# Two queues that fetch single rows: more rows for ScalarE and SyncE, and the rows' offsets loaded earlier

## The chip, the core and the metric

The kernel runs on one core of one Trainium2 chip. Its metric is the device time of one launch in microseconds (us); less is better. Five engines work side by side and meet through semaphores: PE (matrix products), DVE (vector work), ACT (ScalarE: activations), POOL (GpSimd: here it issues gathers by a list of indices) and SP (SyncE: it only issues DMAs). ACT issues DMAs too. Each engine takes its instructions in the program's order.

## What is computed

A recommender's attention over a user's items. For each of B = 16384 users there are 69 item numbers and one label; every number picks a row of 96 floats of a table of 100001 rows. For each of the 69 items the row u, the label's row q and their products go through a small gated layer that gives one weight. The weighted rows are summed in ten groups, and a three-layer network on these sums gives one number for each user.

```python
u = emb[batch_user]                       # 16384 x 69 rows of 96
ql = emb[batch_label[:, 0]]
q = jnp.broadcast_to(ql[:, None, :], u.shape)
z = jnp.concatenate([q, u, q - u, q * u], axis=-1)
h = _dice(z @ W1 + b1, a1, EPS_DICE)      # (alpha * (1 - p) + p) * x, p = sigmoid(x)
att = (h @ W2 + b2) @ W3 + b3
pre = jnp.where(eff, u * att, 0.0)        # eff: batch_user < ITEM_NUM
pooled = jnp.einsum('gf,bfe->bge', window, pre).reshape(u.shape[0], G * E)
x = jnp.concatenate([pooled, ql], axis=-1)
h = _dice(_bn_eval(x @ Wf1 + bf1, EPS_BN), af1, EPS_DICE)
h = _dice(_bn_eval(h @ Wf2 + bf2, EPS_BN), af2, EPS_DICE)
return h @ Wf3 + bf3
```

So 16384 x 69 rows of 384 bytes, picked at random places, have to come from HBM.

## The kernel before, in words

The rows are worked on in chunks of 512: four *tiles* of 128 rows, one row in each partition. There are 32 blocks of 512 users with 69 chunks each, 2208 chunks in all, and the program is written out in 1104 *steps* of two chunks. A table of steps (`plan`, L592) holds what is issued in which step; `at(step, work)` adds to it, and each engine's order follows from the order in which the steps are written out.

In step i the order is: the attention rows of earlier pairs (`rows_of`, every fourth step), the tail chunks of pair i - 3, the spread of weights (every fourth step), the hidden layer of pair i - 2 (`hidden`, L389), ACT's single rows (`scalar_rows`, L610), the pooling of pair i - 7 (`pool`, L448) and the fetch of pair i (`fetch`, L359). A pair's rows stay in one of 15 buffers u (L134) from the fetch until they are pooled, seven steps later.

- **Gathers.** For each tile of a chunk POOL issues one indirect DMA (L266) with 128 indices. PE transposes the tile into PSUM (`ptr`, L325), DVE copies it out (`uT`, L376) and multiplies it by q (`quT`, L379 or L386).
- **The gate.** In `hidden` PE makes `ph` (L396 to L403). ACT makes the sigmoid of it into y (L405) and then `y * (1 - a1) + a1` in place (L406, the identity), and DVE multiplies by `ph` (L407). In the next step PE reads y for the attention rows (`prow`, L414) or a tail (`pa`, L423).
- **Single tiles.** Some tiles, always the fourth of a chunk (`SLOT = 3`), don't go through POOL. Their rows are fetched one by one: `dma_start` of 384 bytes for one partition of a buffer of `ring` (L301). SP fetches 199 such tiles, ACT 170. `SP_CHUNKS` (L52) and `ACT_CHUNKS` (L55) say in which chunk each is read: SP's tile s in step int(5.5 s) + 6, ACT's in step (s + 1) * 128 // 20 + 2. PE waits for the rows by a semaphore of the tile (L320) and then reads the ring's buffer instead of u, for the transpose and again for the pooling. POOL issues no gather for it.
- **The offsets.** The row numbers of single tiles lie in SBUF as byte offsets (`offsets`, L156 to L159). `load` (L283) brings 32 of them at a time into registers of the issuing engine by one instruction (L286, TENSOR_LOAD in the profile), just before the first of the 32 rows that use them. Each row is then a MOVE and a DMA on the engine's queue.
- **When they are issued.** SP's tile s is put into the plan in step int(5.5 s), whole: 128 rows. SP runs free of the steps otherwise: it only waits until the buffer of the ring (eight for SP) has been read out by the pooling of the tile eight before. ACT's rows are spread: 20 in each step, behind the gate's two activations, into a ring of four buffers.

Of the kernel before, what the change touches and what calls it, by code (L numbers as in the profile page):

```python
# [18 lines left out]
P = 128  # L19
# [29 lines left out]

ROW_BYTES = 4 * E  # L50
SLOT = 3
SP_CHUNKS = [2 * (int(5.5 * s) + 6) + 1 for s in range(199)]  # L52
SP_RING = 8
ACT_ROWS = 20
ACT_CHUNKS = [2 * ((s + 1) * P // ACT_ROWS + 2) for s in range(170)]  # L55
ACT_RING = 4
SINGLES = SP_CHUNKS + ACT_CHUNKS
NSB = (len(SINGLES) + P - 1) // P
NSEM = 8
RING_BYTES = 4096  # L60


def chunk_of(c):

    n, k = divmod(c, NCH)
    if n == NBLK - 1 and k >= EARLY:
        k = NMAIN + k - EARLY if k < EARLY + NTAIL else k - NTAIL
    return n, k
# [47 lines left out]
def rec_kernel(  # L116
# [13 lines left out]
    row_bytes = rows.bitcast(U8).rearrange("(o n) k -> o (n k)", o=1)  # L130
# [144 lines left out]
    class Singles:  # L275

        def __init__(self, name, engine, kind, chunks, first, buffers, group):
            self.name, self.engine, self.kind, self.group = name, engine, kind, group
            self.chunks, self.first, self.buffers = chunks, first, buffers
            self.sems = [tc.alloc_semaphore(f"{name}{k}") for k in range(NSEM)]  # L280
            self.given = [0] * NSEM

        def load(self, s, start):  # L283

            i, stop = self.first + s, min(P, start + self.group)
            _, values = nc.values_load_multi_w_load_instructions(  # L286
                offsets[i % P : i % P + 1, i // P, start:stop],
                engines=[self.kind],
                min_val=0,
                max_val=ITEM_NUM * ROW_BYTES,  # L290
                skip_runtime_bounds_check_because="offsets of rows of the table",
            )
            self.values = dict(enumerate(values, start))

        def fetch(self, s, start, stop):

            b, k = self.buffers[s % len(self.buffers)], s % NSEM
            for r in range(start, stop):
                if r % self.group == 0:
                    self.load(s, r)  # L300
                d = self.engine.dma_start(  # L301
                    out=ring[r : r + 1, b], in_=row_bytes[:, bass.ds(self.values[r], ROW_BYTES)]
                ).then_inc(self.sems[k], 16)
                tc.no_tile_sem_insts.add(d.ins.name)
                tc.declare_no_dep(d.ins, group=f"ring{b}", reason="a buffer's readers have waited for its rows")
                fresh.setdefault(b, []).append(d.ins)
            if stop == P:
                for ins in fresh.pop(b):
                    tc.add_to_no_dep_group(f"ring{b}", ins)
                self.given[k] += 16 * P  # L310
                places[self.chunks[s]] = b, self.sems[k], self.given[k]
# [74 lines left out]
                nc.vector.tensor_tensor(quT[:, j, :], ptr, q[:, 0:BLK], ALU.mult)  # L386
        return u, uT, quT

    def hidden(i, uT, quT):  # L389

        ph = ps_h.tile([P, 512], F32, tag="h", name=f"ph{i}")
        places = [chunk_of(2 * i + j) for j in range(2)]
        sums = [ph[j * H1 : (j + 1) * H1, :] for j in range(2)]
        for (n, k), p in zip(places, sums):
            if k >= NMAIN:
                nc.tensor.matmul(p, Cq, qTs[n % 2], start=True, stop=False)  # L396
        for j, ((n, k), p) in enumerate(zip(places, sums)):
            if k < NMAIN:
                nc.tensor.matmul(p, As[n % 2][:, k // 4, :], uT[j], start=True, stop=False)  # L399
            else:  # L400
                nc.tensor.matmul(p, A, uT[j][0:E], start=False, stop=False)  # L401
        for j, p in enumerate(sums):
            nc.tensor.matmul(p, Wp, quT[:, j, :], start=False, stop=True)  # L403
        y = ypool.tile([P, 512], F32, tag="y", name=f"y{i}")
        nc.scalar.activation(y, ph, AF.Sigmoid, scale=S_DICE)  # L405
        nc.scalar.activation(y, y, AF.Identity, bias=a1c, scale=na1c)  # L406
        nc.vector.tensor_mul(y, ph, y)  # L407
        return y
# [131 lines left out]
    pooled, pres, x1s, x2s, qs, us, hs, ys, bands, rws, p1s = ({} for _ in range(11))  # L540
# [26 lines left out]
    def hidden_of(k):  # L567
        return lambda: ys.__setitem__(k, hidden(k, *hs[k]))
# [25 lines left out]
    def at(step, *work):  # L594
        plan.setdefault(step, []).extend(work)

    by_sync = Singles("sp", nc.sync, mybir.EngineType.SP, SP_CHUNKS, 0, range(SP_RING), 32)
    for s, m in enumerate(SP_CHUNKS):
        at(max(0, m // 2 - 6), lambda s=s: by_sync.fetch(s, 0, P))

    by_scalar = Singles(
        "act",
# [1 line left out]
        mybir.EngineType.Activation,  # L604
        ACT_CHUNKS,
        len(SP_CHUNKS),
        range(SP_RING, SP_RING + ACT_RING),
        32,
    )
    def scalar_rows(i):  # L610

        row, stop = i * ACT_ROWS, min((i + 1) * ACT_ROWS, len(ACT_CHUNKS) * P)
        while row < stop:
            s, start = divmod(row, P)
            n = min(P - start, stop - row)
            by_scalar.fetch(s, start, start + n)
            row += n

    c = NPAIR - CLOSE
    for i in range(c):  # L620
        if i >= 3 and (i - 3) % 4 == 3:
            at(i, rows_of(i - 6, 4))
        if i >= 3:
            at(i, tails_of(i - 3))
        if i >= 4 and (i - 4) % 4 == 3:
            at(i, spread_of(i - 7, 4))
        if i >= 2:
            at(i, hidden_of(i - 2))
        at(i, lambda i=i: scalar_rows(i))
        if i < c - CLOSE:  # L630
            if i >= POOL_LAG:
                at(i, pool_of(i - POOL_LAG))
        else:

            for k in {0: (-15, -14), 1: (-13,), 3: (-12, -11), 4: (-10, -9), 7: (-8, -7)}.get(i - c + 8, ()):
                at(i, pool_of(c + k))
        at(i, fetch_of(i))

    at(c, pool_of(c - 6), pool_of(c - 5), tails_of(c - 3), hidden_of(c - 2), fetch_of(c))
# [8 lines left out]
    for n in range(NBLK):  # L648
        first, end = n * NCH // 2, ((n + 1) * NCH - 1) // 2
# [104 lines left out]
```

## Time and profile before

| | |
|---|---|
| time, median of three runs | 16508.57 us (16477.51 to 16532.16) |
| span of the profiled execution, first to last instruction | 10780.4 us |
| between that span and the median | 5728.2 us |
| PE busy | 81% |
| POOL busy | 75% |
| DVE busy | 39% |
| ACT busy (activations alone) | 17% |
| granted clock of PE, mean | 0.749 |
| gathers of u that POOL issues | 8463 |
| single rows issued by SP and by ACT | 25472 and 21760 |

The page gives the span of the profiled execution and no other time of it. The busy shares of POOL and of PE are shares of that span. Instructions that only issue a DMA, move a register or load one are not counted as busy, so SP has no share at all, and ACT's leaves out everything that it issues for the single tiles; their lengths are read from the timeline. The 40 slices of the page are alike from the second to the last but one: there is one stage.

### The profile page before, as it was taken

To read this page: it belongs to the slowest core of one execution; us is meant where nothing else is said; L and a number is where in the kernel's file an instruction comes from. 1 tells how busy PE (TensorE), PEld (TensorE's weight loads), DVE (VectorE), ACT (ScalarE), POOL (GpSimd) and SP (SyncE) were. 2 spreads that over 40 slices of the span, in tenths; PEclk is the share of its full clock that TensorE was granted. 3 is DMA by queue.
4 is the path that set the end of the run, shared out by engine and by line. 5 is a ranking of instruction groups with operands and counts; after the bars stand their busy time and mean duration, and the time that the engine had idled before them with its cause. 6 is when DMAs were issued, how large, how long until landed. Compare 5 with 4: busy or idle time off the path is not lost.

```text
span 10780.4 us, 204439 instructions
## 1 busy us (share of the span) xinstructions
PE 8756.9 (81%) x41797; PEld 4310.8 (40%) x41797; DVE 4235.1 (39%) x7535; ACT 1884.4 (17%) x2761; POOL 8110.8 (75%) x8597
## 2 busy tenths in 40 slices
PE   6888888888887788877888788888887887888888
PEld 3434444434433344433433344333343343443335
DVE  4333333333333333333333343333333334333333
ACT  1111111111111111111111111111111111111112
POOL 7777777777777777777777777777777777777776
PEclk7777777677777777777777777777777777777778
DMA  2222222222222222222222222222222222222221
GB/s 50 42 42 42 45 42 42 42 42 45 42 42 42 45 42 42 42 42 45 42 42 42 42 44 42 42 42 42 44 42 42 42 42 44 42 42 42 42 42 34
DMA packets 372495, 460.70 MB, mean 43 GB/s; under 512 B 232114, under 2 KB 232626, under 8 KB 371106
## 3 DMA queue, kind: packets, MB, share of 16 engines
q0 software_dynamic: 274912, 422.81, 18.9%
q1 hardware_dynamic: 52802, 16.36, 1.0%
q10 hardware_dynamic: 43520, 8.44, 0.7%
q14 instruction: 925, 7.58, 0.2%
q8 instruction: 336, 5.51, 0.2%
HBM read 446.81 MB, written 0.07 MB: 41 GB/s over the span
## 4 chain that ended last, share of the span: by engine, by line
POOL 40%; PE 21%; issue 19%; DMA 12%; ACTq 6%; ACT 2%; DVE 1%; POOLq 0%
POOL u L266 40%; DMA u<-in_rows,ids 12%; ACTq L301 4%; PE acc L325 4%; PE p L502 4%; PE ph L399 3%; PE ph L403 3%; PE ptr L325 2%; PE prow L414 1%; ACTq L286 1%; PE pa L423 1%; ACT y L405 1%; POOL q L266 1%; PE ph L396 1%; PE ph L401 1%
## 5 line engine op out<-in xcount | busy, mean ns | idle before, releaser
L266 POOL DMA_INDIRECT u<-in_rows,ids x8463 | 7989.1, 944 | 2583.5 <-issue 2389.6
L325 PE MATMUL ptr<-ident,u 128*96 128x128 f32 x8463 | 1925.1, 332 | 1606.1 <-DMA u<-in_rows,ids 1555.6
L407 DVE TENSOR_TENSOR y<-ph,y 128x512 f32<-128x512 f32 x1104 | 763.5, 692 | 4972.6 <-ACT y L406 4699.0
L325 PEld LDWEIGHTS acc<-rw,u 128*96 128x96 f32 x15702 | 1674.4, 188 | 1332.5 <-issue 840.4
L325 PEld LDWEIGHTS ptr<-ident,u 128*96 128x96 f32 x8463 | 1131.6, 151 | 2282.7 <-DMA u<-in_rows,ids 1853.2
L325 PE MATMUL acc<-rw,u 128*96 128x20 f32 x15702 | 1792.0, 259 | 212.0 <-DVE rw L436 177.6
L376 DVE COPY uT<-ptr 96x512 f32<-96x512 f32 x2208 | 1489.0, 674 | 739.9 <-PE ptr L325 737.5
L405 ACT ACTIVATE y<-ph 128x512 f32<-128x512 f32 x1104 | 658.8, 597 | 6119.1 <-PE ph L403 3304.1
L399 PE MATMUL ph<-uT,A 128*64 128x512 f32 x4096 | 1598.9, 856 | 0.0
L403 PE MATMUL ph<-quT,wn 96*64 96x512 f32 x4416 | 1540.5, 767 | 0.0
L379 DVE TENSOR_TENSOR quT<-ptr,qT 96x512 f32<-96x512 f32 x2048 | 1379.1, 673 | 0.0
L406 ACT ACTIVATE y<-y,wn,na1c 128x512 f32<-128x512 f32 x1104 | 897.9, 813 | 36.6
L403 PEld LDWEIGHTS ph<-quT,wn 96*64 96x64 f32 x4416 | 429.4, 183 | 1002.5 <-issue 1001.8
L502 PE MATMUL p<-pooled,wf 96*100 96x512 f32 (+1 forms) x1400 | 667.7, 624 | 0.0
L414 PE MATMUL prow<-y,v 128*32 128x512 f32 x2208 | 507.2, 885 | 65.4 <-DVE y L407 57.6
L399 PEld LDWEIGHTS ph<-uT,A 128*64 128x64 f32 x4096 | 259.6, 172 | 609.6 <-issue 605.5
L416 ACT COPY row<-prow 128x512 f32<-128x512 f32 (+1 forms) x277 | 161.6, 583 | 1733.2 <-issue 675.0
L470 DVE COPY pooled<-acc 96x160 f32<-96x160 f32 x1008 | 420.5, 417 | 99.1 <-PE acc L325 97.6
L502 PE MATMUL p<-pre,V 96*100 96x512 f32 (+1 forms) x700 | 398.0, 714 | 11.1 <-DVE x L485 10.8
L502 PEld LDWEIGHTS p<-pooled,wf 96*100 96x100 f32 x1400 | 249.6, 190 | 316.5 <-issue 316.5
L436 DVE SCALAR_TENSOR_TENSOR rw<-patt,bb,wn 128x320 f32<-128x320 f32 x554 | 276.1, 539 | 116.8 <-PE patt L431 114.7
L485 DVE SCALAR_TENSOR_TENSOR x<-p,wf,g 100x512 f32<-100x512 f32 (+3 forms) x105 | 73.9, 704 | 523.6 <-ACT g L484 523.5
(72 smaller groups left out, 2706.1 us busy)
## 6 DMA issues: line engine op xcount, KB each, us to landing
ring<-in_rows SPq DMA_DIRECT2D x25472, 0.4 KB
ring<-in_rows ACTq DMA_DIRECT2D x21760, 0.4 KB
u<-in_rows,ids POOLq DMA_INDIRECT x8463
ids<-in_idx SPq DMA_DIRECT2D x8, 560.0 KB, 3.9
q<-in_emb,ids POOLq DMA_INDIRECT x128
wf<-in_far SPq DMA_DIRECT2D x1, 1209.0 KB, 8.3
wn<-in_near SPq DMA_DIRECT2D x1, 236.0 KB, 3.4
offsets<-in_single_rows SPq DMA_DIRECT2D x1, 192.0 KB, 2.5
```

The lines of the kernel that those rows point to most:

```text
L266: nc.gpsimd.indirect_dma_start(out=dst, out_offset=None, in_=table, in_offset=bass.IndirectOffsetOnAxis(ap=index, axis=0),)
L301: d = self.engine.dma_start(out=ring[r : r + 1, b], in_=row_bytes[:, bass.ds(self.values[r], ROW_BYTES)]).then_inc(self.sems[k], 16)
L325: ins = op(out, ring[:, at[0]].bitcast(F32) if at else u[:, 4 * (c % 2) + t, :], other, **how)
L376: nc.vector.tensor_copy(uT[j][0:E], ptr)
L379: nc.vector.tensor_tensor(quT[:, j, :].rearrange("e (s f) -> e s f", f=FM), ptr.rearrange("e (s f) -> e s f", f=FM), by_field(q[:, k * NS ...
L399: nc.tensor.matmul(p, As[n % 2][:, k // 4, :], uT[j], start=True, stop=False)
L403: nc.tensor.matmul(p, Wp, quT[:, j, :], start=False, stop=True)
L405: nc.scalar.activation(y, ph, AF.Sigmoid, scale=S_DICE)
L406: nc.scalar.activation(y, y, AF.Identity, bias=a1c, scale=na1c)
L407: nc.vector.tensor_mul(y, ph, y)
L414: nc.tensor.matmul(pr[32 * k : 32 * (k + 1), :], v2, ys[b + k], start=True, stop=True)
L502: nc.tensor.matmul(p1, w[:, h * DH : (h + 1) * DH], x, start=(k == 0), stop=(k == KTOP - 1))
```

## The change

Four things are altered, all of them on the single tiles.

- `SP_CHUNKS`: a tile every 5.3 steps instead of 5.5, read 8 steps after it is put into the plan instead of 6; 206 tiles instead of 199.
- `ACT_CHUNKS`: 23 rows a step instead of 20, tiles read 5 steps after their last row's step instead of 2, a ring of 8 buffers instead of 4; 195 tiles instead of 170.
- `load` is called eight rows before the first row that uses its registers (`EARLY_LOAD`), not just before it. The registers of the last eight rows stay valid until then.
- `hidden` takes work that is issued between the gate's two activations: the first four of the step's 23 rows on ACT. The other 19 stand where the 20 stood.

```diff
-SP_CHUNKS = [2 * (int(5.5 * s) + 6) + 1 for s in range(199)]
+SP_STEPS = 5.3
+SP_AHEAD = 8
+SP_CHUNKS = [2 * (int(SP_STEPS * s) + SP_AHEAD) + 1 for s in range(206)]
 SP_RING = 8
-ACT_ROWS = 20
-ACT_CHUNKS = [2 * ((s + 1) * P // ACT_ROWS + 2) for s in range(170)]
-ACT_RING = 4
+ACT_ROWS = 23
+ACT_FIRST = 4
+ACT_AHEAD = 5
+ACT_CHUNKS = [2 * ((s + 1) * P // ACT_ROWS + ACT_AHEAD) for s in range(195)]
+ACT_RING = 8
+EARLY_LOAD = 8
...
             for r in range(start, stop):
-                if r % self.group == 0:
-                    self.load(s, r)
+                g = s * P + r
+                if g == 0:
+                    self.load(0, 0)
+                if (g + EARLY_LOAD) % self.group == 0 and g + EARLY_LOAD < P * len(self.chunks):
+                    self.load(*divmod(g + EARLY_LOAD, P))
...
-    def hidden(i, uT, quT):
+    def hidden(i, uT, quT, between=None):
...
         nc.scalar.activation(y, ph, AF.Sigmoid, scale=S_DICE)
+        if between:
+            between()
         nc.scalar.activation(y, y, AF.Identity, bias=a1c, scale=na1c)
...
-        at(max(0, m // 2 - 6), lambda s=s: by_sync.fetch(s, 0, P))
+        at(max(0, m // 2 - SP_AHEAD), lambda s=s: by_sync.fetch(s, 0, P))
...
-    def scalar_rows(i):
+    def scalar_rows(i, first, last):
 
-        row, stop = i * ACT_ROWS, min((i + 1) * ACT_ROWS, len(ACT_CHUNKS) * P)
+        row, stop = (min(i * ACT_ROWS + n, len(ACT_CHUNKS) * P) for n in (first, last))
...
         if i >= 2:
-            at(i, hidden_of(i - 2))
-        at(i, lambda i=i: scalar_rows(i))
+            at(i, hidden_of(i - 2, lambda i=i: scalar_rows(i, 0, ACT_FIRST)))
+        at(i, lambda i=i: scalar_rows(i, ACT_FIRST if i >= 2 else 0, ACT_ROWS))
```

On ACT's queue, in the middle of the program before: y is the gate's buffer, offsets the loaded row numbers, and the last number of a row DMA's line how many stand one behind the other.

```order
L405 ACTIVATE y_32405<-ph_32400 128x512
L406 ACTIVATE y_32405<-y_32405,wn,na1c 128x512
L301 DMA ring<-in_rows 1x384 x12
L286 TENSOR_LOAD offsets
L301 DMA ring<-in_rows 1x384 x8
L416 COPY row_32523<-prow_32518 128x512
L405 ACTIVATE y_32530<-ph_32525 128x512
L406 ACTIVATE y_32530<-y_32530,wn,na1c 128x512
L301 DMA ring<-in_rows 1x384 x20
```

And two steps of the same stretch now (L311, L292, L415 and L418 are the new numbers of L301, L286, L405 and L406):

```order
L415 ACTIVATE y_33622<-ph_33615 128x512
L311 DMA ring<-in_rows 1x384 x4
L418 ACTIVATE y_33622<-y_33622,wn,na1c 128x512
L311 DMA ring<-in_rows 1x384 x9
L292 TENSOR_LOAD offsets
L311 DMA ring<-in_rows 1x384 x10
L428 COPY row_34141<-prow_34136 128x512
L415 ACTIVATE y_34155<-ph_34149 128x512
L311 DMA ring<-in_rows 1x384 x4
```

Four rows stand between sigmoid and identity, and 19 behind the identity. On SP's queue at the start of the program the loads stood like this, each directly before the 32 rows that use it:

```order
L164 DMA wf<-in_far 128x2418
L286 TENSOR_LOAD offsets
L301 DMA ring<-in_rows 1x384 x32
L286 TENSOR_LOAD offsets
L301 DMA ring<-in_rows 1x384 x32
```

Now the second load stands behind 24 rows, and so on with 32 rows between two loads:

```order
L169 DMA wf<-in_far 128x2418
L292 TENSOR_LOAD offsets
L311 DMA ring<-in_rows 1x384 x24
L292 TENSOR_LOAD offsets
L311 DMA ring<-in_rows 1x384 x32
```

Behind each load but the first there are eight rows whose registers were loaded earlier. The number of loads is one for 32 rows, as before.

More of the change, by code (lines that the diff above doesn't have):

```diff
@@ L281, in __init__ @@
             self.given = [0] * NSEM
+            self.values = {}
         def load(self, s, start):
@@ L292, in load @@
             )
-            self.values = dict(enumerate(values, start))
+            self.values = {g: v for g, v in self.values.items() if g >= s * P + start - self.group}
+            self.values.update(enumerate(values, s * P + start))
         def fetch(self, s, start, stop):
@@ L298, in fetch @@
             for r in range(start, stop):
-                if r % self.group == 0:
-                    self.load(s, r)
+                g = s * P + r
[3 more added lines that the diff above has]
+                    self.load(*divmod(g + EARLY_LOAD, P))
                 d = self.engine.dma_start(
-                    out=ring[r : r + 1, b], in_=row_bytes[:, bass.ds(self.values[r], ROW_BYTES)]
+                    out=ring[r : r + 1, b], in_=row_bytes[:, bass.ds(self.values[g], ROW_BYTES)]
                 ).then_inc(self.sems[k], 16)
@@ L565, in pool_of, with hidden_of @@
         return lambda: pool(k)
-    def hidden_of(k):
-        return lambda: ys.__setitem__(k, hidden(k, *hs[k]))
+    def hidden_of(k, between=None):
+        return lambda: ys.__setitem__(k, hidden(k, *hs[k], between))
     def tails_of(k):
```

## The prediction

> **What bounds the kernel now.** I read the page first, then the groups of GpSimd's instructions, then the waits.
>
> ```profile
> span 10780.4 us, 204439 instructions
> PE 8756.9 (81%) x41797; PEld 4310.8 (40%) x41797; DVE 4235.1 (39%) x7535; ACT 1884.4 (17%) x2761; POOL 8110.8 (75%) x8597
> ```
> ```profile
> L266 POOL DMA_INDIRECT u<-in_rows,ids x8463 | 7989.1, 944 | 2583.5 <-issue 2389.6 <-DMA u<-in_rows,ids 79.4 <-PE ptr L325 78.8
> L266 POOL DMA_INDIRECT q<-in_emb,ids x128 | 121.0, 946 | 40.6 <-issue 38.8 <-DMA ids<-in_idx 1.8
> ```
> ```profile
> POOL u L266 <- issue: 2389.6, 7828, 0.3
> PE ptr L325 <- DMA u<-in_rows,ids: 1555.6, 1927, 2.2
> ```
> By busy share PE leads with 81% and POOL has 75%. The share misleads. A u gather takes 0.944 us and is followed by a pause that is never longer than 0.3 us (the last number of the first wait row), so nothing that the kernel does holds POOL up: it issues without a stop. Busy and idle of the u row make 7989.1 + 2583.5 = 10572.6 us, or 10572.6 / 8463 = 1.249 us for each gather. With the q row (121.0 + 40.6) POOL's gathers fill 10734.2 of the 10780.4 us; 46.2 us are start and tail. PE, with all its work, waits 1555.6 us for gathers to land: 1555.6 / 1104 = 1.41 us in a step. POOL's issue is the bound, and its length is the number of gathers times 1.249 us.
>
> SP and ACT carry single tiles of 128 rows past POOL, one DMA a row. How near are these two queues to their own limit?
>
> ```profile
> 6.74 48.92 SPq L301 DMA_DIRECT2D ring<-in_rows  x128
> ...
> 1189.62 1284.26 SPq L301 DMA_DIRECT2D ring<-in_rows  x3200
> 2474.51 0.37 SPq L151 DMA_DIRECT2D ids<-in_idx  x1
> 2477.15 2.86 SPq L301 DMA_DIRECT2D ring<-in_rows  x9
> ```
> ```profile
> 79.65 0.27 PE L325 MATMUL ptr<-ident,ring 128*96 128x128 f32 x1
> ```
> ```profile
> 10342.04 0.42 PE L325 MATMUL ptr<-ident,ring 128*96 128x128 f32 x1
> ```
> In these rows (start, length, engine) SP works 2477.15 - 1189.62 = 1287.53 us on 25 tiles without a stop: 51.50 us a tile, with its four loads of offsets. PE reads SP's tile 0 (step 6) at 79.65 and tile 192 (step 1062) at 10342.04, so a step lasts 10262.39 / 1056 = 9.718 us, and SP is asked for a tile every 5.5 x 9.718 = 53.45 us. It gains about 2 us a tile.
>
> For ACT, four steps in the middle:
>
> ```profile
> 5003.38 0.60 ACT L405 ACTIVATE y<-ph 128x512 f32<-128x512 f32 x1 [7.97 <-PE ph L403]
> 5004.01 0.81 ACT L406 ACTIVATE y<-y,wn,na1c 128x512 f32<-128x512 f32 x1
> 5004.08 9.05 ACTq L301 DMA_DIRECT2D ring<-in_rows  x20
> 5013.17 0.58 ACT L416 COPY row<-prow 128x512 f32<-128x512 f32 x1 [8.34 <-issue]
> 5015.05 0.60 ACT L405 ACTIVATE y<-ph 128x512 f32<-128x512 f32 x1 [1.30 <-PE ph L403]
> 5015.68 0.81 ACT L406 ACTIVATE y<-y,wn,na1c 128x512 f32<-128x512 f32 x1
> 5015.75 6.37 ACTq L301 DMA_DIRECT2D ring<-in_rows  x20
> 5022.22 0.60 ACT L405 ACTIVATE y<-ph 128x512 f32<-128x512 f32 x1 [5.72 <-PE ptr L325]
> 5022.85 0.81 ACT L406 ACTIVATE y<-y,wn,na1c 128x512 f32<-128x512 f32 x1
> 5022.92 8.85 ACTq L301 DMA_DIRECT2D ring<-in_rows  x20
> 5031.87 0.60 ACT L405 ACTIVATE y<-ph 128x512 f32<-128x512 f32 x1 [8.20 <-PE ph L403]
> ```
> ```profile
> L416 ACT COPY row<-prow 128x512 f32<-128x512 f32 (+1 forms) x277 | 161.6, 583 | 1733.2 <-issue 675.0 <-PE prow L414 487.8 <-PE ptr L325 315.8
> L484 ACT ACTIVATE g<-g,dice,dice 100x512 f32<-100x512 f32 (+3 forms) x105 | 81.5, 776 | 3.5
> L483 ACT ACTIVATE g<-p,dice 100x512 f32<-100x512 f32 (+3 forms) x105 | 68.1, 649 | 732.7 <-issue 248.8 <-PE p L502 166.2 <-PE ptr L325 131.6
> L349 ACT COPY A<-pc 32x512 f32<-32x512 f32 x64 | 35.2, 576 | 248.9 <-issue 127.7 <-PE pc L348 121.2
> ```
> ```profile
> L301 SPq DMA_DIRECT2D ring<-in_rows x25472: 227/228/482, 6.7 to 10349.8; - x199
> L301 ACTq DMA_DIRECT2D ring<-in_rows x21760: 213/214/587, 18.6 to 10606.0; - x200
> ```
> ```profile
> L286 SPq TENSOR_LOAD <-offsets x796: 2025/2176/2410, 4.5 to 10337.5; - x199
> L286 ACTq TENSOR_LOAD <-offsets x680: 2105/2274/2522, 16.3 to 10592.8; - x170
> ```
> Twenty rows without a load take ACT's queue 5022.22 - 5015.75 = 6.47 us, 0.3235 us a row; with a load 5013.17 - 5004.08 = 9.09 and 5031.87 - 5022.92 = 8.95 us, so a load adds 2.55 us. From the sigmoid's start to the first row pass 5004.08 - 5003.38 = 0.70 us in which the queue issues nothing. Summed: 21760 x 0.3235 = 7039, 680 x 2.55 = 1734, 1104 x 0.70 = 773, and 161.6 + 81.5 + 68.1 + 35.2 = 346 for the other activations: 9892 us. ACT's busy share of 17% hides a queue that is 92% full.
>
> **The change part by part.** The sum goes against the profiled execution: its span of 10780.4 us. The median of the runs shown is 16508.57 us, so 5728.2 us lie around the span which no row shows. I take them as constant.
>
> *32 more single tiles.* SP 206 instead of 199, ACT 195 instead of 170: POOL issues 8431 u gathers instead of 8463. 32 x 1.249 = **-40.0 us**, all on the path, since POOL never waits. PE's work is the same, its operand lies in another buffer. SP's and ACT's 4096 added row DMAs run beside POOL as long as both queues keep up. That has to be shown for each, with the new step of 9.718 x 8559 / 8591 = 9.682 us.
>
> *SP, a tile per 5.3 steps.* It is asked for a tile every 5.3 x 9.682 = 51.31 us and needs 51.50 us at the old prices. Its tile 0 is read two steps later than before, at 79.65 + 2 x 9.682 = 99.0, its last (205, step 1094) at 99.0 + 1086 x 9.682 = 10613.7. SP would finish at 6.74 + 206 x 51.50 = 10615.7: about 2 us late at the very end and nowhere else. PE has ten steps left there, in each of which it now waits 1.41 us for POOL, so up to 14 us of lateness is made up: **0 us** in the sum. If this cover goes, each 0.1 us on SP's tile costs 206 x 0.1 = 20.6 us.
>
> *Offsets loaded eight rows sooner.* The load row is 2176 ns (SP) for 32 registers, 68 ns each, and the row DMAs behind a load wait for it: ACT's twenty rows take 2.55 us longer with one, its own row says 2274 ns. Two readings are open. If the sequencer itself is held for the length of the load, its place doesn't matter and nothing is won: 0. If only the first use of a register is held, eight rows of 0.32 us (2.6 us) cover the whole load and SP gains 4 x 2.18 = 8.7 us a tile, ACT 780 x 2.27 = 1771 us in all. No row of this trace has another instruction directly behind a load, so it can't decide; a length that is so even (2025 to 2410) while the rows beside it vary fits a held sequencer, and I take 0. Neither end moves POOL, so the sum doesn't depend on it, only the margin.
> The Trainium skill (Runtime: NRT & Kernel Launch, section Instruction fetch mechanics) puts a register load at about 200 ns a register, even in bulk, because each is a round trip. By it 32 registers would be an estimated 6.4 us and SP's tile 4 x 4.2 = 17 us longer; the trace's 2.18 us decides. Its round trip for each register speaks for the held sequencer, against this part of the change.
>
> *ACT, 23 rows a step, four of them between sigmoid and identity.* Four rows (1.29 us) fill the 0.63 us from 5003.38 to 5004.01 in which the queue stood still, so the gate's cost falls from 0.70 to about 0.07 us (5004.01 to 5004.08). New sum at old prices: 24960 x 0.3235 = 8075, 780 x 2.55 = 1989, 1104 x 0.07 = 77, other 346: 10487 us. The last row stands in step 1085 instead of 1088, so it is wanted three steps before the old 10606.0 and 40 us sooner: about 10537. ACT begins at 16.3, so it would be ready at 10503. **0 us**, with a margin of 34 us, and 27 more that PE can make up in the last 19 steps (19 x 1.41).
> y comes 1.29 - 0.63 = 0.66 us later in each step. Behind it wait DVE's product and PE's tails or rows of the next step. PE can fall behind POOL by 15 - 7 = 8 steps of u buffers before POOL has to wait, so a delay of 0.66 us that doesn't add up costs nothing.
>
> *Rings.* ACT's ring of 8 buffers and the later due steps (5 and 8 ahead instead of 2 and 6) only give the transfers more time; the fourth column of offsets adds 64 KB to one early load. 0.
>
> Sum: 10780.4 - 40.0 = 10740.4 us of span; 16508.57 - 40.0 = **16468.6 us**, 0.24% less. A measurement of this kernel can tell about 0.3% from no change, 49.5 us: the forecast lies inside that.
>
> **The rivals.**
>
> *ACT becomes the bound (slower).* For: the queue would be full to 10487 of about 10520 us, and it has to wait for PE now and then (1.30 us before the sigmoid at 5015.05). Against: a queue that is late doesn't wait, and PE's 1.41 us a step and eight steps of u buffers take up single delays. If a row and a load cost 2% more because both queues issue more, ACT needs 0.02 x 10487 = 210 us more; 61 are covered, 149 come on top of the -40: +109, **16617.6 us**. It decides from 0.6% on (61 us), and makes the kernel slower by more than 49.5 us from (61 + 89.5) / 10487 = 1.4% on.
>
> *SP comes late (no change).* Row DMAs of both queues could hold each other up. For: the longest of SP's row DMAs is 482 ns against a median of 228. Against: the median is the minimum to 1 ns, and the first tile, whose first quarter went out before ACT's first row at 18.6, took 48.92 us with three loads behind its first row, with a fourth some 51.3: hardly less than the later 51.50. If 15% more rows on ACT make SP's tile 0.25 us dearer, it ends 2 + 51.5 us late, 14 are made up, 39.5 us are lost: -0.5, **16508.1 us**.
> The Trainium skill (Perfetto Trace Analysis, section DMA Instruction — HWDGE (DVE, Sync)) says that the descriptor generator is locked for exclusive use while one DMA is prepared and that the wait for it is inside the profiled time: by it this rival would be the likely one. The row's median at its minimum shows that the lock is rarely met.
>
> *The 5728.2 us are not constant.* If the timed runs do the same work stretched by 16508.57 / 10780.4 = 1.531, a gather costs 1.91 us there and 32 of them 61.2 us: **16447.4 us**. For: nothing in the trace explains so much time around the span. Against: nothing in it is stretched either.
> The Trainium skill (Runtime: NRT & Kernel Launch, section The launch sequence) gives about 15 us around a kernel. By that rule most of the difference isn't launch; no row shows what it is.
>
> **How the numbers follow.** Forecast 0.55, ACT 0.12, SP 0.12, stretched runs 0.21. The three runs shown lie up to 31 us from their median, so the forecast, 9.5 us inside the bound, comes out beyond it about three times in ten, and the stretched case (11.7 us outside) about seven in ten: faster 0.55 x 0.3 + 0.21 x 0.7 = 0.31. Slower is the part of the ACT rival beyond 1.4%, 0.10. Same is the rest, 0.59. The range goes from the stretched case less 27 us of scatter, 16420, to the SP rival and the near part of the ACT rival, 16560; beyond it lie most of the ACT rival (0.10) and a little on the low side (0.07).
>
> **What would show it.** Right: POOL has 8431 u gathers with pauses of at most 0.3 us, the span is near 10740, SP's last row is issued at about 10615 and ACT's at about 10500 to 10540. The load is held if its row stays near 2.2 us and the queue issues no row in that time; it is hidden if SP then waits for ring buffers during most of the run. ACT as the bound would show as POOL waits longer than 0.3 us, for PE's reads of u, with PE waiting for DVE's y. SP late would show as PE waiting ahead of its reads of the ring in the last steps. The forecast is wrong if the span differs from 10740 by more than 15 us, or if span and time move by different amounts.

## The result and the profile after

The changed kernel takes 16942.62 us in the median of four runs (16892.35 to 16947.87), the kernel before beside it 16505.62 us (16477.51 to 16532.16): ratio 1.0253, 95% interval 1.0233 to 1.0274. It is slower by 437 us, where 40 us less were forecast.

One thing has to be known ahead of all readings. The kernel before was timed in six jobs; in each all its runs agree, but the jobs fall into two groups, about 10780 us ("short jobs") and 16500 to 16740 us ("long jobs"), and one chip gave 16520.34 us in one job and 10779.24 us in a later one. The pair above and the times that the prediction started from come from one long job, the span of the profile of before belongs to the short ones. So every ratio below is between runs of one job, and the cause of the result has to be looked for twice.

The page of the changed kernel, from a long job; here the time of the profiled run, 16943.73 us, is 1.8 us more than its span:

```profile
span 16941.9 us, 212759 instructions
...
PE 8944.4 (53%) x41797; PEld 4631.8 (27%) x41797; DVE 4187.0 (25%) x7535; ACT 1880.0 (11%) x2761; POOL 8077.2 (48%) x8565
...
L271 POOL DMA_INDIRECT u<-in_rows,ids x8431 | 7955.3, 944 | 8721.6 <-PE ptr L335 3660.8
...
L335 PE MATMUL ptr<-ident,ring 128*96 128x128 f32 x401 | 149.0, 372 | 3905.4 <-DMA ring<-in_rows 3814.3
```

A gather still takes 944 ns, but POOL now stands still for 8721.6 us instead of 2583.5. It waits for PE to read u (3660.8 us of it), and PE in turn waits 3814.3 us ahead of the 401 reads of single tiles, for rows that have not come. By the order of the tiles in `SP_CHUNKS` and `ACT_CHUNKS`, every pause of PE over 0.15 us ahead of such a read stands ahead of a tile of SP, none ahead of one of ACT. Who brings those rows late? Rows of the timeline, SP's queue at the start (start and length in us; the last number counts rows, 128 to a tile):

```profile
7.25 186.61 SPq L311 DMA_DIRECT2D ring<-in_rows  x128
...
194.37 1849.55 SPq L311 DMA_DIRECT2D ring<-in_rows  x2944
```

SP's first tile takes 186.61 us, 48.92 in the profile of before. The next 23 take 1849.55 / 23 = 80.4 us each without a stop, where 51.50 were read before. The chain of waits is SP's queue, and pauses between its instructions ("issue"), nearly throughout:

```profile
SPq 63%; issue 36%; PE 1%; ACTq 0%; ACT 0%; DVE 0%; DMA 0%; another core or an unknown queue 0%
```

In long jobs SP is the bound. In bursts its MOVEs and DMAs stand for about 700 ns each (the 95th of a hundred MOVEs takes 700 ns, the middle one 29), or the next one begins about 700 ns late: on SP's queue 5964 instructions and 5879 pauses last 600 to 900 ns, in the profile of before none and two. Between the bursts a row follows the last after 0.322 us, as before. ACT's queue has such bursts too; gathers and vector work take what they took before, and so, within a few per cent, do the matrix products.

The same kernel in a short job takes 11269.84 us against 10791.34: ratio 1.0443 (1.0425 to 1.0460), 478 us more. There the queues are as quick as in the profile of before, and the waits of POOL read otherwise:

```profile
POOL u L271 <- issue: 2154.6, 6889, 3.2
POOL u L271 <- DMA u<-in_rows,ids: 751.2, 1186, 2.5
POOL u L271 <- PE ptr L335: 119.6, 198, 1.9
```

POOL, which never stood for more than 0.3 us between its gathers of u, now waits 751.2 us for *earlier gathers to land*, up to 2.5 us at a time (the 0.3 us that pass between any two gathers are within it). In the profile of before that row was

```profile
POOL u L266 <- DMA u<-in_rows,ids: 79.4, 260, 0.3
```

and such landings make 37% of the chain in this job, 12% there. So the change makes both groups slower, by two mechanisms that don't occur together. The rest tells them apart.

### The profile page after: what moved, and what is told of

Its sections match the earlier page's. It is cut to its first block, busy times and chain, and to the rows that moved or that the text cites. A ratio compares the mean times of both kernels' runs of the same rounds, so it can differ in the third digit from the quotient of the medians.

```text
span 16941.9 us, 212759 instructions
## 1 busy us (share of the span) xinstructions
PE 8944.4 (53%) x41797; PEld 4631.8 (27%) x41797; DVE 4187.0 (25%) x7535; ACT 1880.0 (11%) x2761; POOL 8077.2 (48%) x8565
## 3 DMA queue, kind: packets, MB, share of 16 engines
q10 hardware_dynamic: 49920, 9.68, 0.4%
## 4 chain that ended last, share of the span: by engine, by line
SPq 63%; issue 36%; PE 1%; ACTq 0%; ACT 0%; DVE 0%; DMA 0%; another core or an unknown queue 0%
SPq L311 54%; SPq L292 9%; ACTq L311 0%; PE acc L335 0%; PE p L514 0%; PE ph L409 0%; PE ph L413 0%; PE ptr L335 0%; ACTq L292 0%; ACT y L418 0%; PE prow L426 0%; SPq L156 0%; DMA wn<-in_near 0%; ACT y L415 0%; DVE y L419 0%
## 5 line engine op out<-in xcount | busy, mean ns | idle before, releaser
L271 POOL DMA_INDIRECT u<-in_rows,ids x8431 | 7955.3, 944 | 8721.6 <-PE ptr L335 3660.8
L335 PE MATMUL acc<-rw,u 128*96 128x20 f32 x15636 | 1944.9, 270 | 1539.2 <-issue 613.9
L335 PEld LDWEIGHTS acc<-rw,u 128*96 128x96 f32 x15636 | 1824.0, 202 | 2651.1 <-issue 1427.1
L335 PE MATMUL ptr<-ident,ring 128*96 128x128 f32 x401 | 149.0, 372 | 3905.4 <-DMA ring<-in_rows 3814.3
L335 PE MATMUL ptr<-ident,u 128*96 128x128 f32 x8431 | 1546.4, 335 | 448.8 <-issue 360.8
L415 ACT ACTIVATE y<-ph 128x512 f32<-128x512 f32 x1104 | 659.0, 597 | 9262.5 <-issue 4292.8
L335 PEld LDWEIGHTS ptr<-ident,u 128*96 128x96 f32 x8431 | 1211.3, 164 | 599.1 <-issue 511.1
L426 PE MATMUL prow<-y,v 128*32 128x512 f32 x2208 | 702.9, 843 | 977.7 <-issue 616.8
L335 PEld LDWEIGHTS ptr<-ident,ring 128*96 128x96 f32 x401 | 61.5, 153 | 3970.5 <-issue 3564.1
L418 ACT ACTIVATE y<-y,wn,na1c 128x512 f32<-128x512 f32 x1104 | 897.4, 813 | 1331.8 <-issue 1062.5
L426 PEld LDWEIGHTS prow<-y,v 128*32 128x32 f32 x2208 | 82.0, 126 | 1308.4 <-issue 877.6
```

What stands on the lines that cost most here:

```text
L271: nc.gpsimd.indirect_dma_start(out=dst, out_offset=None, in_=table, in_offset=bass.IndirectOffsetOnAxis(ap=index, axis=0),)
L335: ins = op(out, ring[:, at[0]].bitcast(F32) if at else u[:, 4 * (c % 2) + t, :], other, **how)
L426: nc.tensor.matmul(pr[32 * k : 32 * (k + 1), :], v2, ys[b + k], start=True, stop=True)
```

## The experiments

Eighteen runs in five jobs. The letters of the theories: S, SP's slow queue is the bound of the timed runs; F, the first profile shows the usual case; A (A1), ACT's queue is too full; A2, the rows inside the gate make y late; D, the single rows of both queues land late beyond a certain rate; D2, late gathers stop POOL only because few of them fit in the ring of descriptors; Q1 and Q2, what makes SP's queue slow in long jobs. "Early loads" are the loads of offsets eight rows sooner.

### Where does the profile of before stand? (short job)

The kernel before, unaltered (e1):

> The kernel before, unchanged, to see an execution whose span goes with its time. Theory S (SyncE is the bound): the span is near 16500, SP's row DMAs take about 16500 / 199 = 83 us a tile instead of the 51.5 us of the first profile, POOL's pauses are longer than 0.3 us and end with PE, which waits for rows of the ring. Theory F (the first profile is typical and some 5.7 ms lie outside the span): span near 10780 again, SP 51.5 us a tile, POOL without a stop.

Measured: 10780.38 us, span 10778.6. Nothing lies around the span but 1.8 us. The 5728.2 us that the prediction took as constant are the difference between a long job and a short one.

### One half of the change at a time (same short job, before 10780.65 us)

ACT's part without SP's (e2), and SP's part without ACT's (e3), both with early loads; then SP with far fewer tiles (e4, made from the kernel before):

```
e2: -SP_STEPS = 5.3   -SP_AHEAD = 8   -range(206)
    +SP_STEPS = 5.5   +SP_AHEAD = 6   +range(199)
e3: -ACT_ROWS = 23 -ACT_FIRST = 4 -ACT_AHEAD = 5 -range(195) -ACT_RING = 8
    +ACT_ROWS = 20 +ACT_FIRST = 0 +ACT_AHEAD = 2 +range(170) +ACT_RING = 4
e4: -int(5.5 * s) + 6 ... range(199)
    +int(8.0 * s) + 6 ... range(136)
```

> The change without SyncE's part: 199 tiles every 5.5 steps, due 6 steps ahead; ACT's 23 rows, the four rows in the gate and the early loads stay. Theory S: the whole loss comes from SP's seven more tiles, so the time goes back to 199 / 206 of 16942, about 16370 to 16510. Theory A (ACT's longer queue is what slows the kernel, through y): the time stays at 16850 to 16950.

Measured: 11125.86 us, ratio 1.0316 (1.0299 to 1.0333): +345 us from ACT's part alone.

> The change without ACT's part: 20 rows a step behind both activations, 170 tiles, ring of four; SP's 206 tiles and the early loads stay. Theory S: ACT doesn't matter, 16900 to 17090 (206 tiles at 82 to 83 us). Theory A: back to 16500 or below.

Measured: 10771.79 us, ratio 0.9991 (0.9982 to 1.0001). Seven gathers fewer at 1.249 us are 8.7 us; 8.9 are seen, with an interval that reaches from 19 us less to 1 us more. Nothing else is seen of SP's part in a short job.

> The kernel before with SP fetching a tile every 8 steps, 136 tiles instead of 199; POOL issues 63 more gathers. Theory S: SP falls from 199 to 136 tiles, 136 x 83 = 11300, and the time falls with it to 11300 or to whatever bounds next (POOL's 8654 gathers x 1.249 = 10810 + 46). Theory F: 63 x 1.249 = 79 us slower than before, about 16585.

Measured: 10854.75 us in one run, +74 us; 63 gathers more at 1.249 us are 79. In short jobs POOL's issue prices a tile that changes its place, as the prediction had it.

The timeline of e2 also shows what a load of offsets does to ACT's queue:

```profile
5022.82 1.14 ACTq L311 DMA_DIRECT2D ring<-in_rows  x4
5024.01 0.81 ACT L418 ACTIVATE y<-y,wn,na1c 128x512 f32<-128x512 f32 x1 [0.97 <-ACT y L415]
5026.49 5.93 ACTq L311 DMA_DIRECT2D ring<-in_rows  x19
5032.53 0.60 ACT L415 ACTIVATE y<-ph 128x512 f32<-128x512 f32 x1 [7.71 <-issue]
```

The load is issued behind the identity at 5024.01, and no row follows until 5026.49, 2.48 us later, though the registers of the next eight rows had been loaded long before. The queue itself is held.

### ACT's part taken apart (another short job, before 10791.34 us)

The whole change again (e5), the gate alone with 20 rows (e6), 23 rows without the gate (e7), early loads alone (e8):

```
e6: -SP_STEPS = 5.3 -SP_AHEAD = 8 -range(206) -ACT_ROWS = 23 -ACT_AHEAD = 5 -range(195) -ACT_RING = 8
    +SP_STEPS = 5.5 +SP_AHEAD = 6 +range(199) +ACT_ROWS = 20 +ACT_AHEAD = 2 +range(170) +ACT_RING = 4
e7: -SP_STEPS = 5.3 -SP_AHEAD = 8 -range(206) -ACT_FIRST = 4
    +SP_STEPS = 5.5 +SP_AHEAD = 6 +range(199) +ACT_FIRST = 0
e8: as e6, and
    -ACT_FIRST = 4
    +ACT_FIRST = 0
```

> The changed kernel unaltered, beside the kernel before on one chip. Where the kernel before takes about 10780 us: theory A (ScalarE's queue is the bound, SP's tiles cost nothing) expects what ScalarE's part alone cost, 11125.86, less 7 gathers of 1.249 us, so about 11117; the forecast's own step (ScalarE free) expects 10740. Where the kernel before takes about 16500 us: theory S (SP's queue is the bound there) expects the ratio of the tiles, 206 / 199 = 1.035 at most, so 16900 to 17080; theory A expects no more than 1.032 too there, so the time alone tells nothing then, only who waits for whom.

Measured: 11269.84 us. Neither number: the forecast's step fails, and theory A is 153 us short. SP's seven tiles, which gained 9 us in e3, cost 478 - 345 = 133 us beside ACT's 23 rows.

> The kernel before with the early loads and with four of ScalarE's twenty rows between sigmoid and identity; tiles, rings and due steps as before. At 10780 us for the kernel before: theory A1 (the queue is too full because of the three rows more in a step) expects 10780, no change, since the gate costs 0.63 us a step less and no row is added; theory A2 (the rows inside the gate make y late in each step and PE waits for it) expects most of the 345 us: 11000 to 11130. At 16500 us for the kernel before, theory S expects no change, since SP's tiles are the same.

Measured: 10786.50 us, ratio 0.9996 (0.9986 to 1.0005). Rows inside the gate do no harm; A2 falls.

> ScalarE with 23 rows a step and 195 tiles, all of them behind the gate, early loads, ring of 8; SP as before. At 10780 us for the kernel before: theory A1 expects more than with the rows in the gate, 10487 + 695 = 11182 us of queue work and the waits on top, 11180 to 11800; theory A2 expects the gate to be harmless again and 10749 (25 gathers fewer). At 16500 us theory S expects no change or the 0.2% of 25 gathers.

Measured: 11427.66 us, ratio 1.0589 (1.0571 to 1.0606): +636 us, 291 more than with the rows in the gate (e2). The saving in the gate is real.

> The kernel before with the offsets loaded eight rows sooner and nothing else. Held sequencer: no change, 10780 (or what the kernel before takes on this chip, within 0.3%), and the span of SP's 25 early tiles as before, 1287 us. Only the first use held: SP's tile 8.7 us shorter, so SP waits for ring buffers; the time stays where POOL is the bound, and falls by up to 17% where SP's queue is.

Measured: 10790.19 us, ratio 0.9998 (0.9989 to 1.0008), and 3200 rows of SP without a stop, with the loads among them, take 1286.62 us; in the kernel before they took 1284.26:

```profile
1188.87 1286.62 SPq L311 DMA_DIRECT2D ring<-in_rows  x3200
```

Loading earlier gains nothing, since the queue is held.

e5 doesn't fit theory A in another way too: in the instruction records ACT's queue in e5 has pauses of over 0.15 us that sum to 1108 of its 11270 us. A queue that waits so long is not the bound. The DMA part of the page says what has become slow. The last number is the time that packets took, as a share of all 16 DMA engines; q0 carries the gathers, q1 SP's rows, q10 ACT's. Kernel before:

```profile
q0 software_dynamic: 274912, 422.81, 18.9%
q1 hardware_dynamic: 52802, 16.36, 1.0%
q10 hardware_dynamic: 43520, 8.44, 0.7%
```

The changed kernel in the short job (e5):

```profile
q0 software_dynamic: 273888, 421.24, 19.9%
q1 hardware_dynamic: 54594, 16.77, 2.6%
q10 hardware_dynamic: 49920, 9.68, 2.1%
```

9% more rows and nearly three times the time: a packet of SP's queue takes 1.0% x 16 x 10780 us / 52802 = 33 ns before and 86 ns now, in the mean of all its packets. Each row leaves two packets, one of 384 bytes and one of 4 (43520 for ACT's 21760 rows); the one of 384 takes 22 ns in the median before and 174 ns in e5. And the 384-byte packets of both queues hardly ever overlap in time (0.6% of them before, 0.8% in e5), as if one engine carried them all. For one engine the shares are 16 times as large: 16 x (1.0 + 0.7) = 27% in the kernel before, with its share of the gathers 46%; in e5 16 x (2.6 + 2.1) = 75%, with gathers 95%. By this sum it is nearly full; the sum counts the time twice in which a row's 4-byte packet overlaps another row's 384. The Trainium skill (DMA: Bandwidth & Descriptors, section Why a DMA increments its semaphore by 16 and not by 1) says that a DMA of SP or ACT that uses k engines runs on the lowest-numbered k of the core's 16, by which all DMAs with k = 1 share one. The trace agrees with one 384-byte packet for each row, so k = 1, and with the 0.8%; it doesn't name the engine of a packet.

In the packet records a row begins to move 0.9 us after its issue (median) in the kernel before, 5.4 us in e5, and 4.6 in e2. A gather adds 16 to its semaphore in single steps, as its shares land. The fifteenth step comes 2.48 us after its issue in the kernel before and 2.49 in e5 (medians), but the sixteenth after 3.35 us before, 7.8 in e2 and 8.7 in e5. So one share of a gather is late by about as much as the rows are, and the other fifteen aren't: the rows stand in the way of one carrier alone.

What does POOL have to do with it? Each gather waits for the semaphore of the gather eight before it, since eight semaphores are used in turn. In e5 no gather starts sooner than 0.26 us after that one has landed, and more than half of the pauses of over 0.6 us end just then. Eight gathers take 8 x 1.249 = 10.0 us, and in e5 a quarter of the gathers need more than 9.9 us to land. That is what POOL waits for. The rows that passed in a us, over the whole span, are 50432 / 11125.0 = 4.533 in e2 and 51328 / 11270.6 = 4.554 in e5. From this comes the limit that theory D was given.

### Theory D against theory A

e9 leaves ACT's part whole and takes tiles from SP; e11 takes one row from ACT; e10 gives the gathers' descriptors twice the room, e12 does so to the kernel before:

```
e9:  -SP_STEPS = 5.3 -SP_AHEAD = 8 -range(206)
     +SP_STEPS = 6.0 +SP_AHEAD = 6 +range(182)
e10: -RING_BYTES = 4096
     +RING_BYTES = 8192
e11: as e2, and
     -ACT_ROWS = 23 -range(195)
     +ACT_ROWS = 22 +range(187)
```

> The changed kernel with all of ScalarE's part (23 rows, 195 tiles, four rows in the gate, early loads), but SyncE with a tile per 6.0 steps, 182 tiles: 377 single tiles in all, 48256 rows, against 369 and 47232 in the kernel before. Where the kernel before takes about 10785 us: theory D (the single rows of both queues go through one DMA path that takes no more than about 4.54 rows a us: 50432 / 11125.0 = 4.533 and 51328 / 11270.6 = 4.554 in the two runs with late rows) expects 48256 / 10775 = 4.48 rows a us to pass, as the 4.47 of the run with SyncE's part alone did: POOL is the bound, 8 gathers fewer, about 10775 (10760 to 10800), rows land 0.9 us after their issue. Theory A (ScalarE's queue is too full) expects what ScalarE's part cost with 199 tiles on SyncE: about 11126, since SyncE's rows don't matter to it.

> The changed kernel with 8192 instead of 4096 bytes for the descriptors of GpSimd's gathers, so that more gathers can be in flight. Theory D expects the rows to stay the bound: 51328 / 4.554 = 11271, within 60 us, and POOL's waits for gathers to go elsewhere (to u buffers, or PE to the ring). Theory D2 (the rows only make a gather land at 3.1 us instead of 2.2, and POOL stops because few gathers fit in the ring) expects POOL to run on: 10740. Theory A expects 11270 too.

> ScalarE with 22 instead of 23 rows a step (187 tiles), four of them in the gate, SyncE as before (199 tiles): 386 tiles, 49408 rows. Theory D expects 49408 / 4.54 = 10883 (10850 to 10910), rows late. Theory A (ScalarE's queue is the bound at 23 rows with 11126) expects the queue's work to fall by 1024 rows of 0.325 and 32 loads of 2.29 us, 406 us, and so POOL to be the bound again: 10765.

> The kernel before with 8192 bytes for the descriptors of the gathers: all theories expect no change, since POOL hardly waits for gathers there (79.4 us in all). It shows what the bytes alone do.

This was a long job (before 16735.22 us), so it doesn't decide between A and D, but tells of long jobs. Measured: e9 15880.86 us, ratio 0.9489 (0.9467 to 0.9511); e10 17162.96, 1.0249 (1.0227 to 1.0271); e11 16790.98, 1.0028 (1.0017 to 1.0038); e12 16730.47, 0.9995 (0.9984 to 1.0006). There the time goes with SP's tiles: 199 with ACT's 22 rows cost 0.3%, 206 with ACT's 23 rows cost 2.5%, 182 with the same 23 rows gain 5%. A tile has no fixed price, though: with 182 tiles the time is 15880.86 / 182 = 87 us a tile, with 206 it is 83. PE's wait for single rows in e12:

```profile
PE ptr L325 <- DMA ring<-in_rows: 4069.0, 188, 47.5
```

and in e9:

```profile
PE ptr L335 <- DMA ring<-in_rows: 1757.0, 125, 36.9
```

The next job was a long one too (before 16520.34 us). With ACT's single tiles gone (e13, range(170) to range(0) in the kernel before) and e9 and e11 again:

> The kernel before with SyncE's 199 tiles and none on ScalarE: 170 gathers more on GpSimd (8633). Where the kernel before takes about 10785 us: 170 x 1.249 = 212 us more, 10997 (all theories; GpSimd is the bound). Where it takes about 16500 to 16750 us and the instructions of SyncE and ScalarE stand for 0.7 us each in bursts: theory Q1 (they stand because both queues issue rows at once) expects SyncE's tile to fall to 51.5 us and the time to 10997 there too; theory Q2 (SyncE's queue is slow there by itself) expects SyncE to stay the bound, 16000 or more.

> The changed kernel with ScalarE's part whole and 182 tiles on SyncE, once more, for a chip where the kernel before takes about 10785 us: theory D (no more than 4.53 to 4.55 single rows a us pass) expects 48256 rows to pass at 4.48 a us: POOL-bound, 10775 (10760 to 10800), rows landing 0.9 us after their issue. Theory A (ScalarE's queue is too full) expects about 11126. At 16500 to 16750 us for the kernel before: 0.949 of it, as before.

> ScalarE with 22 rows a step (187 tiles), four in the gate, SyncE as before (199 tiles): 386 tiles, 49408 rows, once more, for a chip where the kernel before takes about 10785 us: theory D expects 49408 / 4.54 = 10883 (10850 to 10910), rows late by microseconds; theory A expects 406 us less queue work than at 23 rows and so 10765. At 16500 to 16750 us for the kernel before: no difference beyond 0.5%, as before.

Measured: e13 15532.60 us, ratio 0.9390 (0.9367 to 0.9413); e14 15672.72, 0.9481 (0.9465 to 0.9497); e15 16575.08, 1.0031 (1.0020 to 1.0041). e13's chain of waits, with no row left on ACT:

```profile
SPq 63%; issue 35%; PE 1%; another core or an unknown queue 0%; DMA 0%; DVE 0%; ACT 0%; ACTq 0%
```

SP's tile still takes 15532.6 / 199 = 78 us. Q1 falls: SP's queue is slow in long jobs by itself, ACT's rows add only some 5 us a tile to it.

The last job was a short one (before 10779.24 us): e9 and e11 a third time, and a kernel that leaves all tiles but one to POOL (e18).

> The changed kernel with 182 tiles on SyncE and ScalarE's part whole (48256 single rows), a third time for a chip where the kernel before takes about 10785 us: theory D (at most 4.53 to 4.55 single rows a us pass) expects 10775 (10760 to 10800) and rows that land 0.9 us after their issue; theory A (ScalarE's queue is too full) expects about 11126. At 16500 to 16750 us for the kernel before: 0.949 of it, as before.

Measured: 10890.95 us, ratio 1.0103 (1.0086 to 1.0120): between the two theories. ACT's part is that of e2, and 17 tiles fewer on SP take 345 - 112 = 233 us away, which theory A can't give. But D's 10775 fails as well. The windows of e16 (POOL's busy time and number of gathers, granted clock, DMA share, GB/s) show why:

```profile
500.00:1500.00 1000.00, 699.80 (x743) 0.73 0.25 41
2500.00:3500.00 1000.00, 744.39 (x789) 0.77 0.24 42
6000.00:7000.00 1000.00, 743.75 (x788) 0.78 0.24 43
```

743 gathers in the second half millisecond and the third, 788 and 789 later, which is POOL's full pace (789 in the kernel before). POOL falls 98 us behind up to 2000 us and 25 in all the rest, and just up to there the rows start 4.5 to 6 us after their issue (medians of 500 us). My number took the mean rate. At the start SP runs without a stop, 128 / 51.50 = 2.49 rows a us, and ACT 23 / 9.68 = 2.38: 4.86 together. Once its ring is full SP keeps to a tile per six steps, 4.58 together, and the delay falls to between 0.9 and 3.3 us.

> 22 rows a step and 187 tiles on ScalarE, 199 on SyncE (49408 single rows), a third time: theory D expects 49408 / 4.54 = 10883 (10850 to 10910), theory A 10765, where the kernel before takes about 10785. At 16500 to 16750: 1.003 of it, as before.

Measured: 10935.52 us, ratio 1.0140 (1.0123 to 1.0157). D's 10883 is 53 us short, A's 10765 misses by 170. 49408 / 10935.52 = 4.518 rows a us. Its DMA part:

```profile
q0 software_dynamic: 274368, 421.98, 20.4%
q1 hardware_dynamic: 52802, 16.42, 2.5%
q10 hardware_dynamic: 47872, 9.29, 2.1%
```

16 x (2.5 + 2.1) + 20.4 = 94% of one engine, about as in e5.

> The kernel before with a single tile on SyncE and none on ScalarE: 8831 gathers on GpSimd. Its queue needs 8831 x 1.249 + 46 = 11076 us, whatever SyncE and ScalarE do. Where the kernel before takes about 10785, 368 x 1.249 = 460 us of that are lost on the change of place: 11240 by the pauses of GpSimd alone (10780 + 460). Where it takes 16500 to 16750: if the slow instructions of SyncE and ScalarE are the whole difference between the two kinds of chip, 11240 there too, a third less; if these chips are slow in another way as well, 13000 or more.

Measured: 11231.48 us, ratio 1.0416 (1.0398 to 1.0433). 368 gathers more at 1.249 us are 460 us; 452 are seen.

```profile
L266 POOL DMA_INDIRECT u<-in_rows,ids x8831 | 8336.6, 944 | 2691.2 <-issue 2513.8
```

(8336.6 + 2691.2) / 8831 = 1.249 us again.

What holds, then. In short jobs the single rows have a limit, somewhere between 4.55 and 4.7 rows a us:

| kernel | rows asked for in a us, whole span | rows passed in a us, whole span | passed, 500 to 1500 us | passed, 5500 to 7500 us | row's delay, median | time against before |
|---|---|---|---|---|---|---|
| before | 4.38 | 4.38 | 4.54 | 4.55 | 0.9 us | |
| e3, SP's part | 4.47 | 4.47 | 4.54 | 4.54 | 0.9 us | -9 us |
| e16, 182 tiles on SP | 48256 / 10770 = 4.48 | 4.43 | 4.71 | 4.54 | 4.5 to 6 us, then 0.9 to 3.3 | +112 us |
| e17, ACT 22 rows | 49408 / 10759 = 4.59 | 4.52 | 4.68 | 4.64 | 2 to 6 us | +156 us |
| e2, ACT's part | 50432 / 10749 = 4.69 | 4.53 | 4.71 | 4.65 | 2 to 6 us | +345 us |
| e5, the change | 51328 / 10740 = 4.78 | 4.55 | 4.71 | 4.68 | 4 to 6 us | +478 us |

"Asked for" is the number of rows over the time that POOL's gathers alone would need. The two stretches are counted in the packet records. In a stretch 4.54 to 4.55 rows a us pass on time beside 0.80 gathers; where the rows are late by several us, 4.64 to 4.71 pass beside 0.75 to 0.80 gathers. The means over the whole span are no limit: they are lower because the rows end before the span does (in e2 SP's last goes out at 10708.1 and ACT's at 10938.5 of 11125.0 us). So theory D, which took 4.54 from such means, had the mechanism, but no sound number for e16 and e17. Beyond the limit rows start late, a gather's share on the same carrier lands with them, POOL has to wait for the gather eight before, and the steps stretch until the rates agree. e7 is mixed: up to 3000 us its rows are late by 4.6 to 6.5 us, later they are hardly late (0.9 to 1.2 us), and POOL waits for PE instead (408.9 us in all, up to 11.1): there ACT's queue, without the gate's saving, is too full, as rival 1 had it (57% of its chain is ACT's queue).

Not settled: what makes SP's and ACT's instructions stand for 0.7 us in long jobs (only that ACT's rows aren't the cause), and how a kernel without single tiles fares there, which wasn't tried. Nor does any run in a long job have SP's seven tiles alone. Whether a larger ring of descriptors helps in a short job (D2) wasn't run either, since e10 met a long one; but POOL's wait for the gather eight before is a wait for a semaphore, and e10 uses the same eight. No kernel here is faster in both kinds of job: e3 can't be told from before in a short one and had no long one, and e9, 5% faster in long jobs, is 1% slower in short ones.

## Why the prediction was wrong

1. **"5728.2 us lie around the span which no row shows; I take them as constant."** This step failed first. Every run has 1.8 us around its span, so 5728.2 us can't lie there; the timed runs were another regime, and profile and times should not have been added up. The rival that doubted it took a uniform stretch, with gathers at 1.91 us; the page after shows none: a gather takes 944 ns in the long job too, and only the instructions of SP and ACT stand longer.
2. **SP: "asked for a tile every 51.31 us and needs 51.50 us at the old prices", 0 us.** In long jobs a tile takes 82 to 83 us (16505.62 / 199, 16942.62 / 206), SP is the bound and not POOL, and seven tiles more cost 437 us, 62 each. The rival "SP comes late" had the mechanism, PE waiting ahead of its reads of the ring, and where it would show; its price of 0.25 us a tile against 31 was too small by a factor of a hundred. The change hands seven tiles to the queue that is the bound there, and so it is slower; e9 and e14, with ACT's part whole and 17 tiles fewer on SP than before, are faster.
3. **"SP's and ACT's 4096 added row DMAs run beside POOL as long as both queues keep up."** In short jobs the queues keep up (from row to row ACT takes 0.3247 us in e5 and 0.3268 before, means of the instruction records) and the transfers don't. I counted what the rows cost those who issue them and not those who carry them. 478 us in e5 against -40 + 0. The page of before has the row for it, 1.0% and 0.7% of 16 engines being 27% of one, but this gave no warning of the size: with the gathers' share the sum rises from 46% to 95% for 9% more rows. What fails is an overlap that was taken as free: rows and one share of each gather use one carrier, and the gather's last step comes 8.7 us after its issue instead of 3.35.
4. **ACT, 10487 us of queue work, "with a margin of 34 us".** The work was sized 3% too high: without its pauses of over 0.15 us ACT's queue has about 10160 us in e5. Gate: right, e7 against e2. Rival 1 named ACT as the bound; with the rows in the gate ACT isn't it (1108 us of pauses in e5, and e16 falls with SP's tiles), without them it is (e7).
5. **y 0.66 us later, absorbed by u buffers:** right (e6, 0.9996).
6. **Early loads, 0:** right, by the reading taken (e8, and the 2.48 us in e2).
7. **32 gathers at 1.249 us:** the price is right wherever POOL is the bound (e4 74 for 79, e18 452 for 460; e3's 8.9 for 8.7 lies within its scatter). In the changed kernel POOL isn't the bound in either kind of job, so nothing of the 40 us is seen.

Both signs that were to show it wrong came: the span differs from 10740 by far more than 15 us, and span and time moved by different amounts (16941.9 - 10780.4 = 6161.5 us against 437). POOL's pauses also pass the 0.3 us that a right forecast needed.

## What to carry to other kernels

Here a profile's span and the timed runs, 10780 and 16508 us, were not one regime, while within one run they differ by 1.8 us: find the execution that has both before any sum is made. Work that is handed from one engine to two others has three costs, the issuing queues', the giver's, and that of whoever carries the transfers; here the single rows of both queues share a single carrier, so read the share of their DMA queues times 16, and don't take what is left for room (46% became 95% for 9% more rows). Look at the delay from issue to packet too. Near such a limit look at the rate in each stretch and not at the mean, since a stage at the start can be over it alone.

## What the runs showed of the hardware

- Single-row DMAs of 384 bytes of SP and ACT pass on time at 4.55 rows a us in all, beside 0.80 gathers a us: a row starts 0.9 us after its issue (before, e3). At 4.64 to 4.71 rows a us, beside 0.75 to 0.80 gathers, they start 2 to 6 us after it (e17, e2, e5).
- Such rows delay one of a gather's sixteen shares and not the other fifteen: the sixteenth step of its semaphore comes 8.7 us after the issue in e5 instead of 3.35, the fifteenth after 2.49 instead of 2.48.
- The 384-byte packet of a row takes 174 ns in the median of e5 instead of 22 (86 ns instead of 33 in the mean of all packets of SP's queue).
- A load of 32 offsets holds the queue that issues it for about 2.2 to 2.5 us, whether its registers are needed at once or not (2.48 us in e2; e8 gains nothing).
- One kernel can take 10780 or 16520 us on the same chip in two jobs 16 minutes apart, with all runs of a job within 1%. In the long ones the MOVEs and DMAs of SP and ACT, and the pauses between them, last 0.7 us in bursts, while POOL's 944 ns and ACT's activation of 597 ns are unchanged.
